# A four-layer graph network on one core: another way to finish the last unit of layer 3

## The chip, the cores and the metric

The kernel runs on one core of one Trainium2 chip. The metric is the device time of one execution in microseconds (us); the number that counts is the median over several runs of the same kernel on the same chip. The profile is one further execution, taken by the hardware profiler.

The core has five engines that run side by side, each with its own queue of instructions: TensorE (PE; its weight loads are listed as PEld), VectorE (DVE), ScalarE (ACT), GpSimd (POOL) and SyncE (SP), which here only issues DMAs. They meet through semaphores.

## The reference

The input is x of shape (32, 512, 64), 32 samples of 512 nodes with 64 features, and adj, a symmetric normalised 512 x 512 adjacency. Four layers follow each other, each of the form x = x + layer(relu(layernorm(x))). Layers 0 to 2 are a graph convolution, two propagation steps and a graph attention. Layer 3, where the change lies, is an attention with eight heads and an output attention of the same kind:

```python
def gat_layer(x, graph, W, b):
    h = x @ W
    s = jnp.einsum('bnd,bmd->bnm', h, h) * graph
    s = jnp.where(s == 0.0, NEG_INF, s)
    a = jax.nn.softmax(s, axis=2)
    return jnp.einsum('bnm,bmd->bnd', a, h) + b

heads = jax.vmap(lambda W, b: gat_layer(flow_x, graph, W, b))(Wh, bh)
cat = ...                      # the eight heads side by side
x = jax.nn.leaky_relu(cat, negative_slope=0.01)
out = gat_layer(x, graph, W_out, b_out)
return jax.nn.leaky_relu(out, negative_slope=0.01)
```

## The kernel before, in words

Everything is float32. The kernel is written as a fast form, with tests of its assumptions on the data; a flag `again` says at the end whether a general form has to compute everything again (it does not here, but every engine reads the flag and jumps over that code at the end).

Layers 0 to 2 take the first 460 us or so. Layer 3 is then a row of 144 units. A unit is two attention matrices of 512 x 512 that are worked on together: `Heads` units hold two heads of one sample (128 of them), `Out` units hold the output attention of two samples b and b+1 (16 of them, b = 0, 2, ..., 30). The order of the units is a list, `flow`. The last eight are all `Out` units: the seven with b = 16 to 28, and at the very end the one with b = 30.

A unit goes through a row of stages, and `period(t)` (in `planned`) writes one stage of each of about ten successive units into the engines' queues. The order within an engine is the order of these calls (a manual schedule), so an instruction that waits holds back all that stands behind it on its engine. `unit(lag)` is the unit that entered lag periods earlier. The stages of a unit, in order:

- `scores`: for each block r of 128 rows (four blocks), TensorE multiplies into PSUM (`s_ps`, L428).
- `maxima`: DVE adds the mask `flow_neg`, takes the row maxima (`top`) and writes the logits to SBUF (`p`, L443).
- `spread_out`, `spread_in`: the maxima go to DRAM as a row (`top_row`, L450) and come back spread over all partitions (`topb`, L461). Both are DMAs on SP. The matrix of scores is symmetric, so a column's maximum is its row's.
- `shift`: POOL subtracts `topb` (L467, L471); `exps`: ACT takes the exponential (L480). `join`: DVE adds block 0 to block 1 and block 2 to block 3 (L483).
- `make_v`: an `Out` unit turns its feature matrix on TensorE into `gV` (L685, L687) and forms `gD`, differences of neighbouring blocks, on DVE (L689).
- `totals`: TensorE sums the columns with a matrix of ones (`tot_ps`, L501), ACT copies (`tot`, L507). `totals_out`: two DMAs, one on ACT's queue and one on SP's, gather the sums to few columns (`parts`, L512).
- `values`: TensorE multiplies the weights with gV and gD into `av` (L489). There is one buffer for `av`.
- `recips`, `recips_out`, `recips_in`: DVE adds the parts and inverts them (`rec_flow`, L518, L521), SP writes them to DRAM (`rec_row`, L525) and reads them back spread over partitions (`recb`, L532).
- `normalize`: DVE multiplies `av` by `recb` (`o_att`, L538).
- `bias`: ACT adds the output bias and reorders the columns (L716). `back`: TensorE turns the result in four transposes (`back_ps`, L726), ACT forms the scaled copy (L731); `back_dve`: DVE takes the maximum, which is the leaky relu (L734); `back_pool`: POOL adds x (L740); `store`: SP issues two stores (L747).

PSUM tiles of `make_v`, `totals`, `back` and the final test share two buffers (tag "m").

The nodes of a sample are stored with four neighbouring nodes on one partition. The columns of a unit before the change are in the nodes' order, so that a column n = 4i + c belongs to partition i, and copies with `by_blocks` or `in_blocks` change between that order and the order by blocks, in which column 128c + i stands for the same node.

The final test (`any_zero`, L751 to L776) reduces the smallest numbers seen on DVE, turns them on TensorE three times (L756) with reductions on DVE in between, and writes `again`. It is called in period len(units) + 1, as the last call.

Of the kernel before, what the change touches and what calls it, by code (L numbers as in the profile page):

```python
# [14 lines left out]
P = 128  # L15
# [7 lines left out]
def fast_form(  # L23
# [217 lines left out]
    def by_blocks(row):  # L241
        return row.rearrange("p (i c) -> p c i", c=C)

    def in_blocks(row):
        return row.rearrange("p (c i) -> p c i", c=C)
# [118 lines left out]
    class Pair:  # L364
# [27 lines left out]
        def make_v(self):  # L392
            pass
# [4 lines left out]
        def bias(self):  # L398
            pass
# [33 lines left out]
        def maxima(self, r):  # L433
            if r == 0:
                self.begin()
            ps = self.s_ps.pop(r)
            at = (C * self.at + r) % RING
            self.p[r] = (
                lasting[at] if at < len(lasting) else pbuf.tile([P, 2, N], F32, name="p_att")
            )  # L440
            for k in range(2):
                at = k * C + r
                nc.vector.tensor_tensor_reduce(  # L443
                    out=self.p[r][:, k], in0=ps[k], in1=flow_neg[:, r], scale=-1.0,
                    scalar=BIG, op0=OP.add, op1=OP.min, accum_out=self.top[:, at : at + 1],
                )

        def spread_out(self):
            self.top_row = dram.tile([2, N], F32, name="top_row")
            nc.sync.dma_start(  # L450
                self.top_row.rearrange("k (p c) -> p k c", c=C),
                self.top.rearrange("p (k c) -> p k c", k=2),
            )
# [42 lines left out]
        def totals(self):  # L496
            ps = ps_m.tile([P, N], F32, name="tot_ps", tag="m")
            for e in range(2):
                for k in range(2):
                    q = (2 * k + e) * 32  # L500
                    nc.tensor.matmul(  # L501
                        ps[q : q + 32, :], lhsT=ones, rhs=self.p[2 * e + 1][:, k],
                        start=True, stop=True,
                    )
            self.tot = wk.tile([P, N], F32, name="tot", bufs=1)
            self.parts = tiny.tile([P, 2, 8], F32, name="parts")
            nc.scalar.copy(self.tot, ps)  # L507

        def totals_out(self, e, queue):

            rows = self.tot.rearrange("(k e r) n -> k e r n", k=2, e=2)
            queue.dma_start(  # L512
                self.parts[:, e], rows[:, e, 0].rearrange("k (g i) -> k g i", i=8)
            )

        def recips(self):
            self.rec = tiny.tile([P, 8], F32, name="rec_flow")
            nc.vector.tensor_reduce(  # L518
                self.rec, self.parts.rearrange("p e i -> p i e"), AX.X, OP.add
            )  # L520
            nc.vector.reciprocal(self.rec, self.rec)  # L521

        def recips_out(self):
            self.rec_row = dram.tile([2, N], F32, name="rec_row")
            nc.sync.dma_start(  # L525
                self.rec_row.rearrange("k (g i) -> (k g) i", i=8), self.rec
            )
# [8 lines left out]
        def normalize(self):  # L536
            self.o = wk.tile([P, N], F32, name="o_att")
            nc.vector.tensor_tensor(self.o, self.av, self.recb, OP.mult)  # L538

    class Heads(Pair):  # L540
# [106 lines left out]
        def terms(self):  # L647
            return self.g, self.x
# [7 lines left out]
    class Out(Pair):  # L656
# [88 lines left out]
        def store(self):  # L745
            for k in range(2):
                nc.sync.dma_start(  # L747
                    out[self.b + k].rearrange("(p c) f -> p c f", c=C), self.y[:, :, k]
                )

    def any_zero():  # L751

        def across(src, rows, name):
            ps = ps_m.tile([P, P], F32, name=name, tag="m")
            n = src.shape[0]
            nc.tensor.transpose(ps[:rows, :n], src, ident[:n, :n])  # L756
            return ps[:rows, :n]

        own = tiny.tile([P, 1], F32, name="own")
        nc.vector.tensor_reduce(own, least, AX.X, OP.min)  # L760
        two = tiny.tile([1, 2], F32, name="two")
        nc.vector.tensor_reduce(two[:, 0:1], across(own, 1, "own_ps"), AX.X, OP.min)
        best = tiny.tile([B // 2, 2], F32, name="best")
        nc.vector.tensor_reduce(
            best,
            across(least_out, B // 2, "out_ps").rearrange("b (k f) -> b k f", k=2),
            AX.X, OP.max,
        )
        worst = tiny.tile([B // 2, 1], F32, name="worst")
        nc.vector.tensor_reduce(worst, best, AX.X, OP.min)  # L770
        nc.vector.tensor_reduce(
            two[:, 1:2], across(worst, 1, "worst_ps"), AX.X, OP.min
        )
        flag = tiny.tile([1, 1], F32, name="flag")
        nc.vector.tensor_reduce(flag, two, AX.X, OP.min)
        nc.vector.scalar_tensor_tensor(  # L776
            again, flag, 0.0, unsound, op0=OP.is_equal, op1=OP.max
        )
# [6 lines left out]
    def planned(units, products):  # L785

        class Nothing:
            def __getattr__(self, name):
                return lambda *args: None

        nothing = Nothing()

        def period(t):
            def unit(lag):
                return units[t - lag] if 0 <= t - lag < len(units) else nothing


            now, ahead, last = (unit(i) if t - i >= EARLY else nothing for i in (0, -1, 1))
            made = unit(1) if t > 1 else nothing
            summed = unit(2) if t > 2 else nothing  # L800
            for r in range(2, C):
                now.scores(r)
            unit(3).recips_in()
            unit(6).store()
            unit(4).bias()
            last.shift(0, nc.gpsimd)
            made.exps(0)
            summed.totals()
            summed.totals_out(1, nc.scalar)
            u, h = products.get(t - 1, (None, 0))  # L810
            if u and h == H - 1:
                u.keep_product()
            last.shift(2, nc.gpsimd)
            made.exps(2)
            for r in range(2, C):
                now.maxima(r)
            now.spread_out()
            if t == EARLY + 1:
                last.shift(1, nc.vector)
                last.shift(3, nc.vector)  # L820
            summed.totals_out(0, nc.sync)
            now.spread_in()
            for r in range(2):
                ahead.scores(r)
            unit(4).y_pe()
            unit(4).y_act()
            unit(3).normalize()
            for r in range(2):
                ahead.maxima(r)
            unit(4).back()  # L830
            unit(4).y_dve()
            unit(4).back_dve()
            if t != EARLY + 1:
                last.shift(1, nc.gpsimd)
            made.exps(1)
            for j in range(C):
                summed.values(j)
            u, h = products.get(t, (None, 0))
            if u:
                u.product(h)  # L840
            unit(2).recips()
            unit(2).recips_out()
            made.join(1)
            if t != EARLY + 1:
                last.shift(3, nc.gpsimd)
            made.exps(3)
            unit(5).back_pool()
            unit(-2).make_gs()
            made.join(3)
            unit(-3).features(3)  # L850
            unit(-2).judge_product()
            unit(1).make_v()
            unit(-4).make_hx()
            unit(-2).make_g()
            unit(-2).copy_g()
            for step in range(3):
                for lag, odd in ((step - 7, 0), (step - 11, 1)):
                    u = unit(lag)
                    if getattr(u, "i", None) == 0 and u.b % 2 == odd:
                        u.features(step)  # L860
            if t == len(units) + 1:
                any_zero()

        return period

# [2 lines left out]
    products = {}  # L868
    late = []
    for b in range(0, B, 2):  # L870
        out_unit = Out(b)
        for i in range(H // 2):
            pair = [Heads(b + k, i) for k in range(2)]
            for k in range(2):
                u = pair[k]
                u.pair = pair
                flow.append(u)
                if k:
                    for e in range(2):
                        products[len(flow) + 3 + e] = out_unit, 2 * i + e  # L880
                if due and len(flow) >= due[0][0]:
                    v = due.pop(0)[1]
                    (flow if v.b < B - 2 - 2 * LATE else late).append(v)
        due.append((len(flow) + LATE, out_unit))
# [1202 lines left out]
```

## Time and profile before

| | us |
|---|---|
| runs | 2012.55, 2015.15, 2016.46 |
| median of these | 2015.15 |
| the profiled execution's own time | 2012.36 |
| its span (first to last instruction) | 2010.6 |
| PE busy (matmul) | 1950.3 (97%) |
| DVE busy | 1740.0 (87%) |
| POOL busy | 1442.0 (72%) |
| ACT busy | 1322.4 (66%) |

The mean granted clock of TensorE is 0.989 of full speed. The page of a profile has the busy time of each engine, the span in 40 slices, the DMA queues, the chain of waits that ended last, and the costliest groups of instructions. A line of the timeline has the start in us from the span's start, the duration, the engine, the line of the kernel, the operation, what it writes and reads, how many instructions were merged, and in brackets how long the engine had been idle before it and what ended that. A float32 product is recorded as two passes, a transpose as one.

### The profile page before, as it was taken

The page shows a single profiled execution, that of the slowest core. Times are in us where ns is not written, and L with a number is a line of the kernel's source. Part 1 is how long each engine was busy: PE and PEld are TensorE (multiplying, and loading weights), DVE is VectorE, ACT ScalarE, POOL GpSimd, SP SyncE. Part 2 cuts the span into 40 slices and gives each one's busy share as a digit, 9 for nine tenths or more (in the row PEclk, how much of TensorE's full clock was granted, in tenths as well). Part 3 has the DMA queues.
Part 4 walks back from the last instruction along what each step waited for, and adds up shares of the span by engine and source line. Part 5 has one row for each costly group of instructions (what it writes and reads, how often), then busy time and mean ns, then how long its engine had stood idle before and what let it go on. Part 6 is the DMA issues. An engine that isn't in the chain of part 4 may idle for free.

```text
span 2010.6 us, 29032 instructions
## 1 busy us (share of the span) xinstructions
PE 1950.3 (97%) x9338; PEld 728.6 (36%) x9338; DVE 1740.0 (87%) x4109; ACT 1322.4 (66%) x2008; POOL 1442.0 (72%) x832
## 2 busy tenths in 40 slices
PE   7999999979999999999999999999999999999996
PEld 4655554423333333333333333333333333333332
DVE  6799986988898898898889898888888888988994
ACT  3455554536777777777676777767777776766674
POOL 2000000027899999989898989899898898888996
PEclk9999999989999999999999999999999999999998
DMA  4000000002223232322233322332232222222323
GB/s 124 1 1 1 1 1 0 12 24 68 79 72 82 77 85 71 86 76 76 80 81 70 86 74 77 80 81 70 78 78 70 76 72 79 76 70 81 76 76 81
DMA packets 185873, 128.03 MB, mean 64 GB/s; under 512 B 124984, under 2 KB 130272, under 8 KB 185584
## 3 DMA queue, kind: packets, MB, share of 16 engines
q1 hardware_dynamic: 166480, 125.30, 23.3%
q10 hardware_dynamic: 18720, 0.59, 0.5%
q8 instruction: 75, 1.23, 0.3%
q14 instruction: 86, 0.70, 0.1%
q0 software_dynamic: 512, 0.20, 0.1%
HBM read 119.48 MB, written 5.37 MB: 62 GB/s over the span
## 4 chain that ended last, share of the span: by engine, by line
PE 78%; POOL 7%; DVE 6%; DMA 5%; ACT 2%; issue 2%; SPq 0%; ACTq 0%; POOLq 0%; DVEq 0%
PE s_ps L428 21%; PE av L489 20%; PE nt_ps L980 8%; PE tot_ps L501 6%; PE y_ps L624 5%; PE gT_ps L669 5%; PE g_ps L601 3%; PE acc L1096 3%; POOL row L467 2%; POOL p_att L467 2%; DMA topb<-top_row 2%; PE po L1002 1%; DVE row L443 1%; PE den L1107 1%; DMA top_row<-top 1%
## 5 line engine op out<-in xcount | busy, mean ns | idle before, releaser
L428 PE MATMUL s_ps<-g,hx 64*128 64x512 f32 x2048 | 521.1, 618 | 19.9 <-DVE top L443 13.2
L467 POOL TENSOR_TENSOR row<-row,topb 128x1024 f32<-128x1024 f32 x182 | 429.9, 2383 | 0.0
L467 POOL TENSOR_TENSOR p_att<-p_att,topb 128x1024 f32<-128x1024 f32 x182 | 429.9, 2384 | 0.0
L443 DVE CUSTOM_DVE_ANT_0 p_att<-s_ps,flow_neg 128x512 f32<-128x512 f32 x492 | 310.4, 687 | 50.0 <-PE s_ps L428 43.4
L443 DVE CUSTOM_DVE_ANT_0 row<-s_ps,flow_neg 128x512 f32<-128x512 f32 x496 | 312.6, 686 | 38.9 <-PE s_ps L428 38.5
L428 PEld LDWEIGHTS s_ps<-g,hx 64*128 64x128 f32 x2048 | 177.2, 187 | 330.0 <-DVE top L443 186.8
L471 POOL TENSOR_TENSOR p_att<-p_att,topb 128x512 f32<-128x512 f32 x124 | 156.2, 1281 | 75.4 <-DMA topb<-top_row 63.6
L1229 POOL TENSOR_TENSOR x<-x,bias_b 128x512 f32<-128x512 f32 x16 | 20.4, 1278 | 255.6 <-DVE hn L921 255.6
L642 DVE SCALAR_TENSOR_TENSOR cat<-y_ps,bh,cat 128x512 f32<-128x512 f32 x256 | 180.1, 746 | 15.1 <-ACT cat L634 13.4
L471 POOL TENSOR_TENSOR row<-row,topb 128x512 f32<-128x512 f32 x120 | 151.0, 1280 | 58.7 <-DMA topb<-top_row 50.9
L618 ACT COPY g<-g_ps 128x512 f32<-128x512 f32 x128 | 131.8, 1138 | 84.8 <-PE g_ps L601 84.8
L634 ACT ACTIVATE cat<-y_ps,bh 128x512 f32<-128x512 f32 x256 | 161.4, 682 | 34.9 <-PE y_ps L624 34.3
L480 ACT ACTIVATE row<-row 128x1024 f32<-128x1024 f32 x126 | 133.4, 1059 | 69.7 <-POOL row L471 35.5
L480 ACT ACTIVATE p_att<-p_att 128x1024 f32<-128x1024 f32 x123 | 130.3, 1060 | 68.1 <-POOL p_att L471 34.1
L483 DVE TENSOR_TENSOR p_att<-e_ps,p_att 128x1024 f32<-128x1024 f32 x123 | 145.3, 1198 | 13.2 <-ACT e_ps L480 12.9
L483 DVE TENSOR_TENSOR row<-e_ps,row 128x1024 f32<-128x1024 f32 x122 | 144.2, 1197 | 13.4 <-ACT e_ps L480 13.2
L480 ACT ACTIVATE e_ps<-p_att 128x1024 f32<-128x1024 f32 x123 | 125.7, 1029 | 34.4 <-POOL p_att L467 28.3
L480 ACT ACTIVATE e_ps<-row 128x1024 f32<-128x1024 f32 x122 | 124.7, 1029 | 31.7 <-POOL row L467 25.0
L467 POOL TENSOR_TENSOR adj_p<-adj_p,topb 128x1024 f32<-128x1024 f32 x60 | 143.1, 2385 | 0.0
L624 PE MATMUL y_ps<-o_att,wh_sb 64*128 64x512 f32 x512 | 136.8, 594 | 0.0
L669 PE MATMUL gT_ps<-cat,wo_sb 128*64 128x512 f32 x512 | 131.6, 592 | 0.0
L980 PE MATMUL nt_ps<-adj_t,hn 128*128 128x512 f32 x256 | 119.0, 609 | 4.8 <-DVE unsound L272 3.0
(239 smaller groups left out, 3442.6 us busy)
## 6 DMA issues: line engine op xcount, KB each, us to landing
topb<-top_row SPq DMA_DIRECT2D x284, 256.0 KB
recb<-rec_row SPq DMA_DIRECT2D x288, 128.0 KB
out_dram<-y SPq DMA_DIRECT2D x32, 128.0 KB
x<-in_x_dram SPq DMA_DIRECT2D x3, 1024.0 KB
top_row<-top SPq DMA_DIRECT2D x144, 4.0 KB
parts<-tot SPq DMA_DIRECT2D x144, 4.0 KB
parts<-tot ACTq DMA_DIRECT2D x144, 4.0 KB
rec_row<-rec_flow SPq DMA_DIRECT2D x144, 4.0 KB
```

The costliest lines, as they stand in the source:

```text
L428: nc.tensor.matmul(ps[k], lhsT=x[halves(k), r * P : (r + 1) * P], rhs=g[halves(k), :], start=True, stop=True,)
L443: nc.vector.tensor_tensor_reduce(out=self.p[r][:, k], in0=ps[k], in1=flow_neg[:, r], scale=-1.0, scalar=BIG, op0=OP.add, op1=OP.min, accum ...
L467: engine.tensor_tensor(self.p[r], self.p[r], self.topb, OP.subtract)
L471: engine.tensor_tensor(p, p, self.topb[:, k], OP.subtract)
L480: nc.scalar.activation(to, self.p[r], AF.Exp, scale=-1.0)
L483: nc.vector.tensor_tensor(self.p[r], self.joined.pop(r), self.p[r - 1], OP.add)
L489: nc.tensor.matmul(self.av[halves(k), :], lhsT=self.v(k, j) if j % 2 else self.less_next(k, j), rhs=self.p[j][:, k], start=(j == 0), stop= ...
L624: nc.tensor.matmul(ps, lhsT=wh_sb[halves(k), 2 * self.i + k, :], rhs=self.o[halves(k), :], start=True, stop=True,)
L634: nc.scalar.activation(self.cat[:, k], self.y[k], AF.Identity, bias=bh01[:, h : h + 1], scale=0.01)
L642: nc.vector.scalar_tensor_tensor(self.cat[:, k], self.y[k], bh[:, h : h + 1], self.cat[:, k], op0=OP.add, op1=OP.max,)
L669: nc.tensor.matmul(self.gps[halves(k), :], lhsT=wo_sb[:, h, :], rhs=Heads.cat.pop((self.b + k, h)), start=(h == 0), stop=(h == H - 1),)
L980: nc.tensor.matmul(p, lhsT=lhs(k), rhs=adj_t[:, k, :], start=(k == 0), stop=(k == C - 1))
```

## The change

Only the last unit (b = 30) becomes a new class, `Last`; all others stay. For it:

- Its columns are in the order by blocks from the scores on. The scores use `gs` on both sides, the mask is read through a strided view (`seen`), and the maxima are written to DRAM in blocks, `k (c p)` instead of `k (p c)`.
- The sums of its columns are formed by TensorE with the weights as the stationary side and one column of ones as the moving side (`own_sums`), so that they stand on partitions, in PSUM. This is done in two halves: blocks 0 and 1 in `make_v`, blocks 2 and 3 in `recips`, behind the values. DVE adds the halves and inverts them (`own_rec`). `totals`, `totals_out`, `recips_out` and `recips_in` issue nothing for it, save a small load of the output bias into `b_row` on SP.
- `normalize` is a plain copy on ACT. The undivided values are turned, and `back_dve` then divides, adds the bias, takes the maximum and adds x, all on DVE; `back_pool` does nothing.

The final test is called in period len(units), before the turn of the unit that is four periods old, instead of at the end of the next period. In the general `maxima` the operands get views that for all other units come to the same addresses.

```diff
                 nc.vector.tensor_tensor_reduce(
-                    out=self.p[r][:, k], in0=ps[k], in1=flow_neg[:, r], scale=-1.0,
+                    out=in_blocks(self.p[r][:, k]), in0=in_blocks(ps[k]), in1=self.seen(r),
+                    scale=-1.0,
                     scalar=BIG, op0=OP.add, op1=OP.min, accum_out=self.top[:, at : at + 1],
                 )
+        def seen(self, r):
+            return in_blocks(flow_neg[:, r])
...
+    class Last(Out):
+        def totals(self):
+            self.b_row = wk.tile([P, F], F32, name="b_row", bufs=1)
+            nc.sync.dma_start(
+                self.b_row,
+                bass.AP(tensor=b_out.tensor, offset=b_out.offset, ap=[[0, P], [1, F]]),
+            )
+        def totals_out(self, e, queue):
+            pass
+        def terms(self):
+            return self.gs, self.gs
+        def seen(self, r):
+            return by_blocks(flow_neg[:, r])
+        def spread_out(self):
+            self.top_row = dram.tile([2, N], F32, name="top_row")
+            nc.sync.dma_start(
+                self.top_row.rearrange("k (c p) -> p k c", c=C),
+                self.top.rearrange("p (k c) -> p k c", k=2),
+            )
+        def own_sums(self, e):
+            for c in range(C):
+                for k in range(2):
+                    at = 2 * (2 * c + k) + e
+                    nc.tensor.matmul(
+                        self.sums[:, at : at + 1],
+                        lhsT=self.p[2 * e + 1][:, k, c * P : (c + 1) * P],
+                        rhs=ones[:, :1], start=True, stop=True,
+                    )
+        def make_v(self):
+            super().make_v()
+            self.sums = ps_m.tile([P, 4 * C], F32, name="own_sums", tag="m")
+            self.own_sums(0)
+        def recips(self):
+            self.own_sums(1)
+            self.rec = wk.tile([P, 2 * C], F32, name="own_rec", bufs=1)
+            nc.vector.tensor_reduce(
+                self.rec, self.sums.rearrange("p (c e) -> p c e", e=2), AX.X, OP.add
+            )
+            nc.vector.reciprocal(self.rec, self.rec)
+        def recips_out(self):
+            pass
+        def recips_in(self):
+            pass
+        def normalize(self):
+            self.o = wk.tile([P, N], F32, name="o_att")
+            nc.scalar.copy(self.o, self.av)
+        def bias(self):
+            pass
+        def back(self):
+            self.ps = ps_m.tile([P, C, 2, F], F32, name="back_ps", tag="m")
+            for c in range(C):
+                nc.tensor.transpose(self.ps[:, c], self.o[:, c * P : (c + 1) * P], ident)
+            y = row_pair("y")
+            self.y, self.w = (
+                y[:, k].rearrange("p (c k f) -> p c k f", k=2, c=C) for k in range(2)
+            )
+        def back_dve(self):
+            flat = self.w.rearrange("p c k f -> p (c k) f")
+            nc.vector.tensor_tensor(
+                flat, self.ps.rearrange("p c k f -> p (c k) f"),
+                self.rec[:, :, None].to_broadcast([P, 2 * C, F]), OP.mult,
+            )
+            nc.vector.tensor_tensor(
+                flat, flat, self.b_row[:, None, :].to_broadcast([P, 2 * C, F]), OP.add
+            )
+            nc.vector.scalar_tensor_tensor(
+                self.y, self.w, 0.01, self.w, op0=OP.mult, op1=OP.max
+            )
+            for k in range(2):
+                nc.vector.scalar_tensor_tensor(
+                    self.y[:, :, k], self.y[:, :, k], -1.0,
+                    xs[self.b // G][:, self.b % G + k], op0=OP.add, op1=OP.add,
+                )
...
             for r in range(2):
                 ahead.maxima(r)
+            if t == len(units):
+                any_zero()
             unit(4).back()
...
-            if t == len(units) + 1:
-                any_zero()
...
-        out_unit = Out(b)
+        out_unit = (Last if b == B - 2 else Out)(b)
```

More of the change, by code (lines that the diff above doesn't have):

```diff
@@ L749, in store, with back_pool @@
                 )
+    class Last(Out):
[58 more added lines that the diff above has]
+                flat, self.ps.rearrange("p c k f -> p (c k) f"),
+                self.rec[:, :, None].to_broadcast(
+                    [P, 2 * C, F]
+                ),
+                OP.mult,
+            )
[10 more added lines that the diff above has]
+                )
+        def back_pool(self):
+            pass
```

## The prediction

> **What bounds the kernel now.** I read the page first, for the engines and the DMA queues; then the chain of waits over the last 26 us; then the timeline of the same stretch, engine by engine; then a table of 3.41 us windows for TensorE's clock. The edit touches only the last unit (the pair b=30, 31; I call the units by their b: 24, 26, 28, 30) and the place of the final test. So the page says little about it: over the span the chain is TensorE's, and a few microseconds at the end are 0.1 to 0.2 per cent of it.
>
> ```profile
> q10 hardware_dynamic: 18720, 0.59, 0.5%
> ...
> PE 78%; POOL 7%; DVE 6%; DMA 5%; ACT 2%; issue 2%; SPq 0%; ACTq 0%; POOLq 0%; DVEq 0%
> ```
>
> In the last stretch the chain leaves TensorE. It runs from the last join through unit 30's row sums into three DMAs (first column start, second duration, us):
>
> ```profile
> 1986.60 1.24 DVE row L483
> ...
> 1987.88 1.82 PE tot_ps L501 x4
> ...
> 1989.73 0.59 ACT tot L507
> ...
> 1990.34 2.27 DMA parts<-tot
> ```
>
> The timeline shows what follows, one engine at a time, each idle before its turn:
>
> ```profile
> 1989.62 1.11 PE L726 MATMUL back_ps<-ident,o_att 128*128 128x128 f32 x4
> ...
> 1990.66 1.46 PE L489 MATMUL av<-p_att,gD 128*64 128x512 f32 x4
> ...
> 1998.21 0.69 DVE L538 TENSOR_TENSOR o_att<-av,recb 128x512 f32<-128x512 f32 x1 [1.85 <-DMA recb<-rec_row]
> ...
> 1998.94 1.18 ACT L716 ACTIVATE o_att<-o_att,b_out 128x512 f32<-128x512 f32 x1 [1.91 <-DVE o_att L538]
> ...
> 2000.17 1.11 PE L726 MATMUL back_ps<-ident,o_att 128*128 128x128 f32 x4 [3.78 <-ACT o_att L716]
> ...
> 2001.95 0.69 DVE L734 SCALAR_TENSOR_TENSOR y<-back_ps,y 128x512 f32<-128x512 f32 x1 [2.45 <-ACT y L731]
> 2002.78 1.40 POOL L740 TENSOR_TENSOR y<-y,x 128x256 f32<-128x256 f32 x2 [1.73 <-issue]
> ```
>
> The values of unit 30 (L489) are ready at 1994.70, but the division waits until 1998.21 for the reciprocals' trip through DRAM. SP issues the last two stores from 2003.53, the second at 2004.21. The span ends at 2010.6, so 6.4 us follow the last store's issue; the edit leaves them as they are. From the last join's end (1987.84) to that issue are 16.4 us, and this is what the edit rebuilds.
>
> TensorE's clock matters as much as the waits. Columns: window, length, PE busy, PEld, DVE, ACT, POOL, granted clock, DMA share, GB/s.
>
> ```profile
> 1977.81:1981.22 3.41, 2.12 (x12) 0.99 (x12) 0.69 (x1) 2.17 (x4) 3.41 (x3) 1.00 0.44 109
> 1981.22:1984.64 3.42, 3.10 (x16) 1.11 (x12) 1.32 (x4) 2.26 (x3) 3.42 (x2) 1.00 0.06 4
> 1984.64:1988.05 3.41, 1.22 (x6) 0.32 (x8) 2.33 (x3) 2.51 (x3) 3.41 (x5) 1.00 0.37 109
> 1988.05:1991.46 3.41, 3.41 (x10) 1.01 (x8) 0.80 (x2) 1.21 (x3) 0.21 (x1) 0.50 0.19 45
> ```
>
> A window with 1.22 of 3.41 us busy is followed by one at half clock; one with 2.12 is not. The same table has 1.54 us in the window from 1967.57, again followed by half clock. So the line lies between 45 and 62 per cent busy.
>
> **The change part by part.** Times are on the clock of the profiled execution (2012.36 us, span 2010.6); it stands 2.8 us under the median of 2015.15, and I carry differences over to the median.
>
> *Removed from unit 30's path:* tot_ps (1.82 after the join), tot (0.59), parts (2.3), reduce and reciprocal on the gathered sums (0.4), rec_row and recb (1993.14 to 1998.21), the division before the turn (0.7), the bias (1.2). The final adds move from POOL to DVE.
>
> *The final test moves two periods ahead,* between tot_ps of unit 28 and the turn of unit 24. Its first reduction (L760, 0.24) stands on DVE behind unit 26's division, which ends at 1979.93 because its recb arrives at 1979.24. TensorE waits at the test's first transpose until 1980.2. The test's stretch on TensorE and DVE was 1994.62 to 1995.74, 1.1 us. So back_ps of unit 24 starts at 1981.35 instead of 1978.19, and the values of unit 28 behind it at 1982.0 instead of 1980.08 (+1.9). In 1977.81 to 1981.22 TensorE is then busy some 0.8 us (24%), so by the table the next window runs at half clock: another 1.5 us. The values of unit 28 end at 1987.2, not 1983.7. Its cover: unit 30's shifts on POOL end at 1985.5 and its last join at 1987.84, which the test does not touch. Gone is the cover of gV_ps of unit 30, which now ends at 1987.9. On DVE unit 24's y and unit 28's reciprocal come 0.7 us later, and unit 28's division at 1989.2 instead of 1988.46.
>
> *own_sums, first half:* 8 products, in the trace 16 passes, each with a 128-column weight load and one moving column. The nearest row is m_ps (L323, 128x128 weights, 64 columns): 16 passes start between 75.7 and 77.3, 0.107 apart, so 1.9 us with the drain. A floor is half of it, if one column costs less than 64; at half clock the weights cost up to twice as much. I take 1.9: 1987.9 to 1989.8. The turn of unit 26 follows (0.66), and the values of unit 30 start at 1990.55, against 1990.66. What tot_ps gave back is thus spent before the path proper begins.
>
> *Values, second half, turns:* values 3.65 at full clock, ended at 1994.3 (before 1994.70, part of it at half clock); own_sums 1.9, to 1996.2. Then in a row: unit 28's turn 0.66, its ACT pass 0.60, its DVE pass 0.69, each with 0.05 of hand-over: 1998.25. Unit 30's turn is done by then, and so is its copy on ACT (0.6, beside own_sums). The new DVE tail: division as L1161 (0.69, with a broadcast reciprocal), b_row as L223 (0.69), maximum as L229 (0.69), two adds as L1215 (0.42, the second begun 0.36 later), 0.03 between dependent ones: 2.94. The last store is issued at 2001.25 instead of 2004.21: 3.0 us gained.
>
> *top_row of unit 30* is written in 4-byte pieces, 1,024 in place of 256. A small packet costs an engine 0.5% x 16 x 2010.6 / 18720 = 8.6 ns (row q10); 48 more on each of 16 engines are 0.4 us. SP's issue time grows slowly, 0.32 for 128 pieces, 0.38 for 256, 0.55 for 512; I take 0.5 us in all. More pieces cannot shorten it, so the floor is 0. A ceiling is the slope from rec_row (128 pieces, 1.40 us until SP goes on at 1994.54) to this DMA (256, issued 1969.01, SP goes on at 1971.45): 8.1 ns per piece, 6.2 us for 768. Queued behind it on SP: topb of unit 30, then rec_row and recb of unit 26. POOL has 1.2 us of slack for topb (landing near 1974.8, first shift 1976.06); unit 26's division has none (it waited 1.75 us for recb), and the test and the turn stand behind it. So the 0.5 us is on the path: 2.5 us gained.
>
> The Trainium skill speaks against this edit ("DMA: Bandwidth & Descriptors", "Rules for kernel authors"): a strided last dimension becomes one descriptor per element and should be made contiguous. Its bandwidth table gives about 10.5 ns per packet, by which an estimate of the extra is 0.5 us and the sum would hardly differ; that the pieces cost only their packets no run here shows yet.
>
> *With one answer:* the eight maxima read flow_neg at a stride of four; a strided DVE copy (L277) takes 624 ns, less than the 687 of this operation, so nothing, with 0.8 us (four times 0.2, what a stride adds from L219's 422) as the bound. In other units the new views merge into the same flat rows. b_row's DMA precedes unit 24's stores on SP, 0.5 us for which nobody waits; it lands 10 us before its use.
>
> **The rivals.** *Faster:* the test's wait costs no half-clock window, or the one-column passes are cheap. Then unit 28's division (1989.9) starts the values, and the gain is 3.7 us, 4.6 with passes at half the row's price. For it: the windows' phase is not tied to the program. Against it: three microseconds of idling fit no phase easily. Time about 2011.0. *Values at half clock:* if one-column passes don't count as busy, the window from 1988.05 has 1.6 us (47%), and unit 30's values lose 1.7 us: gain about 1, 2014.2. *Slower:* the 4-byte write of top_row at its ceiling. With 6.2 us the division of unit 26, the test and all values behind it move 6.2 us, POOL's shift 5: 3.2 us lost, 2018.3. It decides from 3.0 us on, and costs over 0.2 per cent from 7. For it: SP waits at this DMA each period. Against it: no packet row is over 9 ns at that size.
>
> **How the numbers follow.** About 0.2 per cent, 4.0 us, is what a measurement of this kernel can tell from no change (the runs shown span 2012.55 to 2016.46). The forecast, gain 2.5 in a range of 1.5 to 4, has 0.46; 2015.15 - 2.5 = 2012.65, its own range 2011.1 to 2013.7. Faster rival 0.30, half-clock values 0.10, slower rival 0.14. A gain over 4.0 comes from most of the faster rival (0.27) and, with the spread of the runs, 0.13 of the forecast: 0.40. Slower by over 4.0: 0.08 of the write rival and 0.02 of the rest. Left for within: 0.50. The range goes from 2008.6 (the lowest run, 2012.55, less 4) to 2016.6 (just over the highest run, hardly any gain).
>
> **What would show it.** Right: no tot_ps, rec_row or recb for unit 30; own_sums twice near 1.9 us; a half-clock window while unit 28's values run; the last store issued some 3 us earlier, 6.4 us ahead of the end. Wrong: SP going on from top_row more than 3 us after its issue, POOL waiting for topb; own_sums over 3 us; the values of unit 30 at clock 0.5; DVE's tail over 3.5 us; or a changed start of the last period.

## The result, and the profile after

The changed kernel takes 2032.05 us (median of 5 runs, 2030.26 to 2032.39), the kernel before, run beside it, 2015.62 (5 runs, 2012.55 to 2016.54). The ratio is 1.0082, its 95% interval 1.0071 to 1.0094: 16.4 us slower, where 2.5 us of gain were forecast. The profiled executions took 2032.22 and 2012.36 us, 19.9 apart, since the profiled one of before lies at the low end of its runs.

Two different losses make this up. The first is nowhere near the edit. These are lines of the page after: span, small DMA packets, the chain by engine, and the score products (busy us, mean ns of one, then idle time with its releaser).

```profile
span 2030.3 us, 29716 instructions
...
q10 hardware_dynamic: 18590, 0.59, 0.5%
...
PE 77%; DVE 7%; POOL 6%; DMA 5%; ACT 3%; issue 2%; SPq 0%; ACTq 0%; POOLq 0%; DVEq 0%
...
L428 PE MATMUL s_ps<-g,hx 64*128 64x512 f32 x2048 | 533.1, 626 | 20.5 <-DVE top L443 13.7
...
L428 PEld LDWEIGHTS s_ps<-g,hx 64*128 64x128 f32 x2048 | 181.3, 187 | 337.5 <-issue 294.4
```

The same lines of the page before:

```profile
span 2010.6 us, 29032 instructions
...
L428 PE MATMUL s_ps<-g,hx 64*128 64x512 f32 x2048 | 521.1, 618 | 19.9 <-DVE top L443 13.2
...
L428 PEld LDWEIGHTS s_ps<-g,hx 64*128 64x128 f32 x2048 | 177.2, 187 | 330.0 <-DVE top L443 186.8
```

The score products of the 128 `Heads` units, which the change was said to leave alone, are 12 us longer, and there are 684 more instructions, though the last unit adds some 25 products. The releaser of the weight loads is no longer DVE but "issue": TensorE's queue itself. In the trace's records, TensorE has 730 wait instructions of 51 ns rather than 214, GpSimd 586 rather than 460. The spread-outs (`top_row` on SP, one per unit) slip a little in every unit: 9.1 us between the 9th and the 143rd, against before. That the waits are the reason is tested below.

The second loss is in the last unit. Its chain (start and duration in us):

```profile
1981.33 10.48 DMA top_row<-top
...
1992.73 4.47 DMA rec_row<-rec_flow
...
1997.80 2.88 DMA recb<-rec_row
...
2004.20 6.16 PE av L493 x16
...
2012.68 0.70 DVE o_att L542
...
2013.51 3.65 PE av L493 x16
2017.17 1.88 PE own_sums L788 x16
```

and the timeline of the same stretch (in brackets: idle before it, and what ended that):

```profile
1980.21 1.08 DVE L443 CUSTOM_DVE_ANT_1 row<-s_ps,flow_neg 128x512 f32<-128x512 f32 x1
...
1991.83 0.81 SPq L465 DMA_DIRECT2D topb<-top_row  x2
1992.08 0.17 DVE L522 TENSOR_REDUCE rec_flow<-parts 128x8 f32<-128x16 f32 x1 [9.47 <-DMA parts<-tot]
...
2003.56 2.34 DVE L878 SCALAR_TENSOR_TENSOR again<-flag,unsound 1x1 int32<-1x1 f32 x1
...
2007.83 1.21 DVE L487 TENSOR_TENSOR row<-e_ps,row 128x1024 f32<-128x1024 f32 x1
...
2010.78 1.84 PE L788 MATMUL own_sums<-ones,p_att 128*128 128x1 f32 x16
...
2020.81 0.68 DVE L831 TENSOR_TENSOR y<-back_ps,own_rec 128x512 f32<-128x512 f32 x1
2021.03 1.85 POOL L744 TENSOR_TENSOR y<-y,x 128x256 f32<-128x256 f32 x2 [4.77 <-issue]
2021.53 0.77 DVE L838 TENSOR_TENSOR y<-y,b_row 128x512 f32<-128x512 f32 x1
2022.34 1.10 DVE L841 SCALAR_TENSOR_TENSOR y<-y 128x512 f32<-128x512 f32 x1
2023.47 0.76 DVE L845 SCALAR_TENSOR_TENSOR y<-y,x 128x256 f32<-128x256 f32 x2
```

SP's two issues in the timeline before:

```profile
1969.01 0.38 SPq L450 DMA_DIRECT2D top_row<-top  x1
...
1971.45 0.80 SPq L461 DMA_DIRECT2D topb<-top_row  x2
```

SP issues `top_row` at 1981.33 and goes on with `topb` only at 1991.83, after 10.5 us instead of 2.4. Meanwhile VectorE is idle for 9.47 us, for `parts`: this gather of an earlier unit's sums was issued on SP 0.5 us behind `top_row` (1981.80), and a last semaphore event that fits it stands in the trace at 1991.99. So what was issued behind `top_row` on SP's queue is late with it. The strided maxima run as another form of the operation, of 1.07 to 1.21 us instead of 0.69. The last step of the final test, one element, takes 2.34 us; it took 0.15 before. The last join ends at 2009.04, 27.7 us after `top_row`'s issue; before it was 18.8. From there to the last store's issue it is 15.5 us, before 16.4. In this stretch the values of unit 28 (2004.20, at a mean granted clock of 0.58) take 6.2 us, where they took 3.65 before and 5.2 were forecast, and unit 30's values start behind unit 28's division (2012.68), 4.5 us after the join, where 2.7 were forecast.

The two profiled executions differ by 19.8 us of span: 12.3 until the last `top_row` (10.4 of drift, of which 1.3 is from the start to the ninth unit, and 1.9 from the maxima), 8.9 from there to the last join, -0.9 to the last store, -0.6 behind it.

### The profile page after: what moved, and what is told of

The parts are those of the page before. It is cut to its first block, busy times and chain, and to the rows that moved or that the text cites. A ratio compares the mean times of both kernels' runs of the same rounds, so it can differ in the third digit from the quotient of the medians.

```text
span 2030.3 us, 29716 instructions
## 1 busy us (share of the span) xinstructions
PE 1963.8 (97%) x9362; PEld 741.5 (37%) x9362; DVE 1749.7 (86%) x4112; ACT 1320.5 (65%) x2006; POOL 1439.5 (71%) x830
## 4 chain that ended last, share of the span: by engine, by line
PE 77%; DVE 7%; POOL 6%; DMA 5%; ACT 3%; issue 2%; SPq 0%; ACTq 0%; POOLq 0%; DVEq 0%
PE s_ps L428 21%; PE av L493 20%; PE nt_ps L1082 8%; PE tot_ps L505 5%; PE y_ps L628 5%; PE gT_ps L673 4%; PE g_ps L605 3%; PE acc L1198 3%; POOL row L471 3%; POOL p_att L471 1%; PE po L1104 1%; DMA top_row<-top 1%; DVE row L443 1%; DMA recb<-rec_row 1%; DVE p_att L443 1%
## 5 line engine op out<-in xcount | busy, mean ns | idle before, releaser
L428 PE MATMUL s_ps<-g,hx 64*128 64x512 f32 x2048 | 533.1, 626 | 20.5 <-DVE top L443 13.7
L443 DVE CUSTOM_DVE_ANT_0 p_att<-s_ps,flow_neg 128x512 f32<-128x512 f32 x488 | 308.0, 685 | 47.9 <-PE s_ps L428 40.7
L428 PEld LDWEIGHTS s_ps<-g,hx 64*128 64x128 f32 x2048 | 181.3, 187 | 337.5 <-issue 294.4
L646 DVE SCALAR_TENSOR_TENSOR cat<-y_ps,bh,cat 128x512 f32<-128x512 f32 x256 | 180.0, 745 | 15.5 <-ACT cat L638 14.0
L487 DVE TENSOR_TENSOR row<-e_ps,row 128x1024 f32<-128x1024 f32 x122 | 144.8, 1197 | 14.6 <-ACT e_ps L484 14.2
L484 ACT ACTIVATE e_ps<-row 128x1024 f32<-128x1024 f32 x122 | 124.9, 1030 | 37.4 <-POOL row L471 32.1
L542 DVE TENSOR_TENSOR o_att<-av,recb 128x512 f32<-128x512 f32 x143 | 98.3, 688 | 30.7 <-DMA recb<-rec_row 29.1
```

Of the source, the lines that this page charges most:

```text
L428: nc.tensor.matmul(ps[k], lhsT=x[halves(k), r * P : (r + 1) * P], rhs=g[halves(k), :], start=True, stop=True,)
L443: nc.vector.tensor_tensor_reduce(out=in_blocks(self.p[r][:, k]), in0=in_blocks(ps[k]), in1=self.seen(r), scale=-1.0, scalar=BIG, op0=OP.ad ...
L484: nc.scalar.activation(to, self.p[r], AF.Exp, scale=-1.0)
L487: nc.vector.tensor_tensor(self.p[r], self.joined.pop(r), self.p[r - 1], OP.add)
L646: nc.vector.scalar_tensor_tensor(self.cat[:, k], self.y[k], bh[:, h : h + 1], self.cat[:, k], op0=OP.add, op1=OP.max,)
```

## The experiments

They ran in three groups (runs 1 to 4, 5 to 8 and 9 to 11), each group on another chip, with the kernel before beside it: medians of 2010.9 to 2011.4 us, 21 to 25 runs. Each run is compared with the kernel before of its own group; the row "after, again" is run 10. The one trace of before is that of the first comparison, so that the trace columns compare single executions on different chips. The table has the difference of the medians, the ratio's 95% interval, the drift of `top_row` between the 9th and the 143rd unit against the trace of before, and, from the last unit's first `top_row` issue, the time until SP goes on with topb, until the last join ends and until the last store is issued.

| kernel | us over before | ratio, 95% | drift | topb | join | store |
|---|---|---|---|---|---|---|
| before (first chip's trace) | | | 0 | 2.4 | 18.8 | 35.2 |
| after, again | +14.4 | 1.0060 to 1.0087 | 7.8 | 9.2 | 26.2 | 41.6 |
| 1 views alone | +6.9 | 1.0019 to 1.0043 | 7.6 | 2.8 | 18.8 | 34.8 |
| 2 flat but last | +7.3 | 1.0030 to 1.0058 | 0.9 | 9.3 | 25.4 | 40.0 |
| 3 node order | +3.1 | 1.0007 to 1.0026 | -0.1 | 2.7 | 21.0 | 40.7 |
| 4 test ahead alone | +0.3 | 0.9993 to 1.0011 | -0.3 | 2.5 | 20.9 | 38.0 |
| 5 view on scores | +7.9 | 1.0033 to 1.0060 | 8.8 | 2.7 | 18.8 | 34.9 |
| 6 4-byte rows alone | +3.5 | 1.0009 to 1.0029 | 0.6 | 7.2 | 22.8 | 39.4 |
| 7 node order, test behind | +3.1 | 1.0005 to 1.0023 | 0.9 | 3.2 | 18.9 | 38.7 |
| 8 node order, test in PSUM | +1.8 | 1.0005 to 1.0023 | 0.1 | 2.5 | 18.9 | 37.4 |
| 9 view on rows | -0.7 | 0.9985 to 1.0003 | -0.2 | 2.5 | 18.9 | 35.2 |
| 11 sums by rows | -4.2 | 0.9973 to 0.9991 | 0.1 | 2.7 | 18.8 | 31.9 |

### The views, all together, and all but in the last unit (1, 2)

The first puts the change's views into the kernel before, the second takes them out of all units but the last of the changed kernel.

```diff
-                    out=self.p[r][:, k], in0=ps[k], in1=flow_neg[:, r], scale=-1.0,
+                    out=in_blocks(self.p[r][:, k]), in0=in_blocks(ps[k]),
+                    in1=in_blocks(flow_neg[:, r]), scale=-1.0,
```

> The kernel before, with one edit: all units' maxima are written with the four-block views (out, scores and mask), as the change writes them. The instructions are the same flat rows on every engine; in the built program 520 of the score matmuls now wait for TensorE's own count as well, which puts 517 more wait instructions on TensorE's queue, and GpSimd gets 128 more. Theory A (the views cost time through these waits): the spread-outs of unit after unit drift as in the changed kernel, 10.4 us by the last unit, so 2015.6 + 10.4 = 2026.0 us; 517 waits at 20 ns each would be this much. Rival B (the drift of the changed kernel comes from something in its last unit, for instance its new tiles or its second form of the maxima operation): no drift, 2015.6 us.

> The changed kernel, with flat rows again in the maxima of all units but the last. Theory A: the drift of 10.4 us is gone, so 2032.05 - 10.4 = 2021.6 us; the last unit keeps its own costs (eight maxima at 1.13 rather than 0.69 us, SP held 10.5 rather than 2.4 us by top_row). Rival B: 2032 us, drift as before. What stays above 2015.6 is the last unit's: 6 us by A.

Measured: +6.9 and +7.3 us. The drift comes with the views (7.6) and goes without them (0.9), and nothing of the last unit is needed for it. Theory A holds; its size was 3.5 us too high. Of its 10.4 us, 1.3 were a difference in the start of the two executions, and the drift itself was 9.1 there, 7.6 to 8.8 in the three later traces with views on all units.

### Which view (5, 9)

```diff
 run 5, TensorE's waits only:
+                    out=self.p[r][:, k], in0=in_blocks(ps[k]), in1=in_blocks(flow_neg[:, r]),
 run 9, GpSimd's waits only:
+                    out=in_blocks(self.p[r][:, k]), in0=ps[k], in1=flow_neg[:, r],
```

> The kernel before with the four-block view on the scores and the mask alone (what the maxima read), the written rows flat. In the built program this gives TensorE 517 more wait instructions, and GpSimd none. Theory: TensorE's waits are the whole cost of the views (it is over 97% busy, GpSimd has idle time): 6.9 us over the kernel before on the same chip, as all the views together cost in the run before, with a drift of 7 to 8 us by the last unit. Rival: GpSimd's 128 waits carry it, or both share it by their number: 0 to 3.5 us.

> The kernel before with the four-block view on the written rows alone, scores and mask flat. In the built program this leaves TensorE's waits as they were and gives GpSimd 128 more wait instructions. Theory: GpSimd's waits lie in its idle time: within 2 us of before, no drift. Rival: they cost as TensorE's do, by number 128/517 of 7.9 us, or more: 2 us or more, with a drift to match.

Measured: +7.9 us and -0.7 (no difference). Page of the kernel with the view on the scores:

```profile
span 2016.7 us, 29551 instructions
...
L428 PEld LDWEIGHTS s_ps<-g,hx 64*128 64x128 f32 x2048 | 181.3, 187 | 336.0 <-issue 291.8
```

and with the view on the written rows:

```profile
span 2007.7 us, 29160 instructions
...
L428 PEld LDWEIGHTS s_ps<-g,hx 64*128 64x128 f32 x2048 | 177.1, 187 | 329.1 <-DVE top L443 186.8
```

519 more instructions against 128 more; the releaser "issue" stands only in the first. TensorE's waits are the cost of the views, as far as the runs can tell: 6.9 and 7.9 us of time, or 7.6 and 8.8 of drift, over 517 are 13 to 17 ns each. GpSimd's 128 cost nothing that can be measured (-3.0 to +0.6 us). The view on what the maxima read decides (run 5 has it on the scores and the mask together): the next product into the same PSUM buffer waits for VectorE's read and, with the view, for TensorE's own count as well, and an instruction with a second wait gets a wait instruction ahead of it. The traces' semaphore records agree: at L428, 521 weight loads wait for a count that TensorE itself raises, against 1 before, and 537 wait instructions stand there rather than 17 (runs 1 and 5; in run 9 it is 1 and 17). Whether the time goes into the added instruction or into waiting for that count the runs don't separate. A possible reason, not tested, is that whoever places the waits does not take the view for a read of the whole buffer.

### The 4-byte rows alone (6)

```diff
+            if isinstance(self, Out) and self.b == B - 2:
+                for c in range(C):
+                    nc.sync.dma_start(rows[:, :, c : c + 1], tops[:, :, c : c + 1])
+                return
             nc.sync.dma_start(rows, tops)
```

> The kernel before, where the last unit alone writes top_row in 4-byte pieces: four DMAs of 256 pieces each, in node order, so that the result stays the same. SP is held for the three further issues, 3 x 0.5 = 1.5 us. Theory E (the pieces were mis-sized in the prediction): SP goes on with topb 10 us or more after the first issue, rather than 2.4, and unit 30's last join and the last store come 6 to 8 us later, 6 us over before. Rival (the prediction's 0.5 us; what held SP in the changed kernel was something else, such as the last maxima or a load beside it): SP goes on within 5 us, and the time is within 2 us of before.

Measured: SP goes on 7.2 us after the first issue (1.6 of it for the three further issues), the last join comes 4.0 us later and the last store 4.2, and the time is 3.5 us over before. Theory E has the direction and the mechanism; its sizes were taken from the single DMA of 1,024 pieces and were too high for four of 256. The prediction's 0.5 us is excluded by SP's 7.2, where the rival had at most 5; the interval of the time, 1.8 to 5.8 us, alone would not do it. The trace of the changed kernel shows where the time is not: the 4-byte packets start within 0.7 us, from 1982.2 to 1982.9, at 7 ns each. The sixteen semaphore events that end this DMA come from 1989.81 to 1991.81. So the pieces leave quickly and are long in being reported done. Run 6 adds what this goes with: the first of its four DMAs, 256 pieces of 4 bytes, is reported done 2.3 us after its issue, as 256 pieces of 16 bytes were before (2.4), and the next three 1.8, 1.9 and 1.2 us after one another. So it goes with the number of pieces, some 6 ns each here (4.9 us for 768). Why the report is late no run shows.

### The last unit without strides (3), and the test ahead alone (4)

Run 3 takes the changed kernel with flat rows in all units, `Out`'s own `terms` and `spread_out`, and

```diff
-                        lhsT=self.p[2 * e + 1][:, k, c * P : (c + 1) * P],
+                        lhsT=self.p[2 * e + 1][:, k, c::C],
...
-            nc.scalar.copy(self.o, self.av)
+            nc.scalar.copy(in_blocks(self.o), by_blocks(self.av))
```

Run 4 is the kernel before with `any_zero()` moved alone.

> The changed kernel with the last unit's columns left in node order: maxima flat in all units, the last included, top_row written in rows of 16 bytes as before, own sums from every fourth column of the plain blocks, and the copy of the values puts them into blocks. Neither strided maxima nor a 4-byte top_row are left; own sums, division after the turns and the early final test stay. Theory A (waits 10.4, maxima 1.9, top_row 8.1, the rest about -4): 2032.05 - 10.4 - 1.9 - 8.1 = 2011.7 us, if weights read at every fourth column load as fast as plain ones; with loads of double time some 2 us more. Rival C (top_row's 8.1 us lie beside something else that ends nearly as late, as TensorE's half clock or the values of unit 28): 2016 to 2020 us.

> The kernel before with the final test alone moved, two periods ahead and in front of the turns of unit 26. The prediction has it move the values of unit 28 from 1983.7 to 1987.2 and leave the end of the last join, and so the end of the kernel, where they are: 2015.6 us, within 1 us. Rival D: the half clock that it brings reaches into unit 30's scores or sums, or TensorE's wait reaches the last join: 2 to 4 us slower, 2018 to 2020 us.

(The "unit 26" in the second text is unit 24, as in the prediction.)

Measured: +3.1 and +0.3 us. Node order recovers the maxima and `top_row`, but the gain that theory A had (3.9 us, or 2 with slow loads) is missing. The time is the one that theory C had, 0.4 to 4.4 us over, and the half clock that it named is there (in run 3 unit 30's values take 6.2 us at a mean clock of 0.58). But in both kernels the last join is late as well. Timeline of run 3:

```profile
1981.75 0.14 DVE L860 TENSOR_REDUCE flag<-two 1x1 f32<-1x2 f32 x1
1981.92 4.62 DVE L861 SCALAR_TENSOR_TENSOR again<-flag,unsound 1x1 int32<-1x1 f32 x1
1982.73 2.44 POOL L467 TENSOR_TENSOR row<-row,topb 128x1024 f32<-128x1024 f32 x1
1985.04 1.50 POOL L740 TENSOR_TENSOR y<-y,x 128x256 f32<-128x256 f32 x2
```

The test's last operation ends at 1986.54, in the moment in which GpSimd's row of work ends. VectorE is held for 4.62 us (5.05 in run 4), and the last join ends 2.1 us later. In run 4 alone this costs nothing that the runs can tell (-1.4 to +2.2 us), so theory D is not borne out in time, though something does reach the join; it is VectorE, and not the half clock or TensorE's wait of that theory. Run 4's trace has the last store 2.8 us later behind the last `top_row`, but that `top_row` itself 2.6 us earlier, 1.9 of it already at the ninth unit, so that one trace doesn't settle what the hold is worth.

### The test behind, and the test with one SBUF operand (7, 8)

Run 7 is run 3 with `any_zero()` at its old place; run 8 is run 3 with

```diff
-        flag = tiny.tile([1, 1], F32, name="flag")
+        flag = worst_ps[:, 0:1]
```

> The kernel of the third run (columns of the last unit in node order, own sums, division after the turns), with the final test back at the end of its period. Theory H (the last operation of the early test, one element with two SBUF operands, was held on VectorE for 4.6 us while GpSimd ran on): it runs in 0.15 us, the last join ends 18.8 us after the last top_row's issue rather than 21.0, unit 28's division 4 us earlier, and the time falls from 3.1 us over before to between 0 and 1 us over; it doesn't reach the prediction's gain of 3, since own sums run at half clock here, 3.6 to 3.9 us each rather than 1.9. Rival I: the sums alone hold the end, and the time stays 3 us over.

> The kernel of the third run with the final test still ahead, but its minimum left in PSUM, so that the test's last operation has one SBUF operand rather than two. Theory H (it was held because it reads two SBUF operands while GpSimd runs): 0.15 to 0.2 us for it rather than 4.6, the last join 18.8 us after the last top_row's issue, and 0 to 1 us over before. Rival J (it is held for something else: a semaphore, its int32 result, or VectorE's order): 4.6 us as before, the last join at 21.0, and 3 us over.

Measured: the operation takes 0.15 us in both and the join ends at 18.9. Run 8, at the same place as run 3 and beside a GpSimd as busy:

```profile
1983.26 0.15 DVE L860 SCALAR_TENSOR_TENSOR again<-worst_ps,unsound 1x1 int32<-1x1 f32 x1
```

Theory H holds for the hold, and J falls: with one operand in PSUM it is gone (0.15 us in run 11 too). How long it lasts is another matter. In runs 3 and 4 VectorE was held through the GpSimd instruction that was running and three more; in the changed kernel, and in run 10 (2.22 us), only to the end of the one beside it, though more followed without a gap. In run 2 the same operation with two SBUF operands took 0.16 us, beginning 0.15 us before a GpSimd instruction ended:

```profile
1991.33 0.16 DVE L881 SCALAR_TENSOR_TENSOR again<-flag,unsound 1x1 int32<-1x1 f32 x1
```

What lets it in no run shows. The time does not follow as expected: +3.1 in run 7, which is rival I's number, and +1.8 in run 8. Between runs 3 and 8 the intervals overlap, so the worth of the hold is not resolved. In run 7 the test's three turns now stand behind own sums on the path, 2 us of TensorE. The expectation's reason for the rest, own sums at half clock, was wrong. In run 8 TensorE is at full clock while they run (window, length, PE, PEld, DVE, ACT, POOL, granted clock, DMA share, GB/s), and it is the weight loads that are long:

```profile
1998.00:2001.90 3.90, 3.90 (x19) 3.88 (x18) 0.00 (x0) 0.58 (x1) 0.00 (x0) 1.00 0.31 66
```

```profile
L771 PEld LDWEIGHTS own_sums<-ones,row x16: 309/330/330, 1998.0 to 2001.5; 128*128 128x128 f32 x16
```

330 ns in the middle from every fourth column; in the changed kernel, from plain blocks, 192. Sixteen of them make 3.9 us where 1.9 were forecast, twice over.

### The changed kernel again (10), and sums by rows (11)

> The changed kernel itself, on the chip of these runs, so that the parts can be summed beside it: 16 us over before, as in its first comparison. Parts measured one by one: views 7 to 8, 4-byte rows 3.5, columns in node order with the test ahead 3.1; a sum of 14 to 15 that leaves 1 to 2 for the strided maxima.

Measured: +14.4 us. Runs 1 and 2 split the change in two, the views (6.9) and all the rest (7.3): 14.2 together. Within the rest the parts are less clean. Views 6.9 to 7.9, 4-byte rows 3.5 and node order 3.1 come to 13.5 to 14.5, but this closeness is partly chance: node order has strided weight loads and a longer hold, which the changed kernel has not, and lacks the strided maxima, which it has. The maxima alone were not run; the traces of the changed kernel have 1.9 and 2.0 us for them.

Run 11 is run 8 without own sums from the weights:

```diff
+            super().totals()                     # ones as weights; the copy goes into blocks:
+                nc.scalar.copy(in_blocks(self.tot), by_blocks(ps))
...
+            for c in range(C):
+                nc.tensor.matmul(
+                    self.sums[:, 4 * c : 4 * c + 4],
+                    lhsT=self.tot[:, c * P : (c + 1) * P], rhs=ident[:, 0::32],
+                    start=True, stop=True,
+                )
```

> A version from the findings: the kernel of the eighth run (node order, flat rows, division after the turns, test ahead with its minimum in PSUM), with the row sums made as in the kernel before (ones as weights, 1.8 us), copied into blocks by ScalarE, and brought onto partitions by four small matmuls on that copy in place of own sums (16 weight loads each half, 329 ns each from every fourth column). Theory K (TensorE's 7.8 us of own sums is what keeps the eighth run above before): some 5 us of TensorE's path go, VectorE's last steps start by 29 us after the last top_row's issue, not 33, and the time is 2 to 3 us under before. Rival L (the division of unit 28, or the stores before, end next): within 1 us of before.

Measured: 2007.25 us, 4.2 under before, ratio 0.9973 to 0.9991 (1.8 to 5.4 us): faster than the kernel before and, by 18.6 us, than the changed one in run 10. Its timeline:

```profile
1994.28 1.05 PE L774 MATMUL own_sums<-ident,tot 128*128 128x4 f32 x8
...
1997.11 0.68 DVE L809 TENSOR_TENSOR y<-back_ps,own_rec 128x512 f32<-128x512 f32 x1
```

What remains of the sums behind the values is 1.05 us. VectorE's last steps start 28.2 us after the last `top_row`, and the last store is issued at 31.9 instead of 35.2. Theory K holds, with rather more gain than the 2 to 3 us that it named. So the idea of the change, sums on partitions and the division after the turns, is worth about the 3 us of the forecast when nothing else is paid for it (3.3 us less from `top_row` to the last store in this trace).

## Why the prediction was wrong, step by step

- **"In other units the new views merge into the same flat rows."** This is the step that failed most. The addresses do merge: the maxima of the other units keep their form and their 685 ns. But the step looked at addresses alone, and the waits do not stay the same. It was priced at nothing and is 6.9 to 7.9 us (runs 1 and 5). A count of TensorE's wait instructions (214 and 730 in the two traces) shows the difference; their price had still to be measured.
- **top_row in 4-byte pieces: 0.5 us taken, ceiling 6.2.** This is the second step that failed, mis-sized: SP was held 8.1 us longer, above the ceiling, and 6.8 in run 10. The mechanism of the slower rival is the one that came, and its sign ("SP going on more than 3 us after its issue") appeared. The packet row (8.6 ns each, on sixteen engines) described the packets well, 7 ns, but the wait is for the completion. The slope between two earlier DMAs of 128 and 256 pieces, 8.1 ns per piece, was the nearer row; here it is 8.06 / 768 = 10.5 ns. The Trainium skill's rule ("DMA: Bandwidth & Descriptors", "Rules for kernel authors") spoke rightly against the edit. Its price per packet ("Bandwidth"), about 10.5 ns, was misread: it is the busy time of a whole transfer divided by its 64 packets, and the prediction's 0.5 us divides it by the sixteen engines once more. Undivided it gives an estimate of 768 x 10.5 = 8.1 us, what SP was held here; since the page measured transfers into SBUF that GpSimd issued, the closeness may be chance.
- **Strided maxima: nothing, bound 0.8 us.** Eight times 0.43 us, of which 1.9 reach the last `top_row`. The strided copy from which it was argued is another operation, and the bound took four of the eight.
- **The test ahead: TensorE's wait and a half-clock window, the last join untouched.** The half clock was there, but mostly after the wait for `top_row` (a mean of 0.52 in 1992 to 2001, 0.54 in 2001 to 2010). What was not seen is VectorE held by GpSimd: 2.3 us here, 4.6 and 5.1 in runs 3 and 4, with a join 2.1 us later in these two. The Trainium skill states it ("SBUF — State Buffer", "Who interferes with whom"): a VectorE instruction with two SBUF inputs contends with a GpSimd instruction that reads SBUF, and the ports that the two share are an exclusive lock. Runs 8 and 11 agree with the condition (0.15 us with one input in PSUM). The changed kernel has one instruction's wait, 2.3 us; run 3 goes further, since VectorE was held through three following GpSimd instructions as well.
- **own_sums, 1.9 us each half.** Right: 1.84 and 1.95, from plain blocks at full clock.
- **VectorE's tail, 2.94 us.** 3.4: the addition of the bias and the maximum took 0.77 and 1.10 beside GpSimd's two additions for unit 28, the second of which took 1.17 instead of 0.73. That this is the same contention is argued, not tested.
- **Last join to last store, 3.0 us shorter.** 0.9 shorter here; the values of unit 30 end 8.1 us after the join, forecast 6.5, since those of unit 28 and its division were late (half clock), and the tail takes 0.5 more. The trip through DRAM did leave the path, as run 11 shows at full size.

## What to carry to other kernels

A rewritten access pattern that touches the same bytes can still change the waits, and on an engine that is 97% busy each extra wait counts (13 to 17 ns here, 517 of them): count the wait instructions of both built programs, by engine, before pricing an edit at nothing. A small DMA on the path is priced by its completion, from rows with a like number of pieces, not by its packets. And where an operation is moved, ask what the neighbouring engine does at the new place; here one element on VectorE waited up to 5 us for GpSimd.

## What was not expected of the hardware

- 1,024 pieces of 4 bytes to DRAM leave within 0.7 us and are reported done 6.9 to 8.9 us later.
- A one-element operation with two SBUF operands was held 2.2 to 5.1 us beside GpSimd in four traces, through one GpSimd instruction or through four, and not at all in a fifth (run 2, 0.16 us); with one of them in PSUM, 0.15 us.
- Loading 128 x 128 weights from every fourth column takes 330 ns instead of 192, at full clock.
- The added waits cost TensorE 13 to 17 ns each and GpSimd, with idle time, nothing that can be measured.
